# A first layer whose TensorE order is written out by hand, and W2 prepared from split parts alone

## The chip, the core and the metric

The kernel runs on one core of a Trainium2 chip. The metric is the device time of one execution in microseconds (us). Before the change it is 360.69 us, the median of 3 runs (360.64 to 360.71). Six names recur: PE is the matrix engine (TensorE), PEld its weight loads, DVE the vector engine, ACT the scalar engine, POOL GpSimd, and SP the queue that issues most DMAs.

## The reference: what is computed

Input x is 4 batches of 512 tokens of 256 float32 values. Two layers follow each other; each adds a mixer, multiplied by a gate:

```python
xn = _layernorm(x)
s = _L0_attn_ref(xn, ...)                 # xn + rmsnorm((y(xn @ W_in.T)) @ W_out.T) * norm_w
g = _silu(_L0_ffn_ref(xn, W1, W2, W3))
x = x + s * g
# the second layer: the same, with causal attention as its mixer
# _L?_ffn_ref:
hidden = jax.nn.silu(up_gate) * up_lin    # x @ W1.T, x @ W3.T, 1024 wide
hidden = fwht(hidden)                     # Walsh-Hadamard transform along the 1024
out = jnp.einsum('bsh,dh->bsd', hidden, W2)
```

The first layer's recurrence starts from zero, so its state is one product per channel, and the whole first mixer folds into one 256 x 256 matrix (`m` in the kernel).

## The kernel before, in words

**Split products.** [...] To keep precision every operand is split into a high part, the rounded value, and a low part, the rest. `split` (L59) has ACT make the high part by a cast and DVE the low part by a subtraction. A product is then three products: high x high, high x low, low x high (`mm3`, L80). Operands of 512 columns cost one instruction per 128 rows of contraction.

**Weights.** The Walsh-Hadamard transform is moved into W2 by `prep_w2` (L139): three butterfly steps on DVE over the 8 row blocks, then a product with a 128 x 128 Hadamard matrix on PE (`w2ps`), whose result is split into `w2h` and `w2l`. This is done for two halves of W2's columns in each layer. In the first layer's first half the Hadamard product takes the float32 values unsplit (`native`, with `had_f`); in the other three it takes split parts (`had`). W1 and W3 of the first layer come as four tiles `w13_0` to `w13_3`; each serves two of eight chunks of 128 hidden channels (`split_w13`, L118). `prep_m` (L187) makes `m` from `win` and `wout` (`wg`, `wi`, `mps`).

**The first layer.** `ffn` (L461) runs once for each batch. For each of 8 chunks `c` it makes two up products (`gu`, 12 instructions of 512 columns), a silu on ACT, the gating product `h` on DVE (L523), a split into `hh` and `hl`, and, later, the down product of a chunk (`down`, 12 instructions of 256 columns) into the two banks `dn`. Before, a down runs one chunk late (`defer=1`); in batch 0 all downs come at the end (`defer=NH`), since W2 isn't ready. After each chunk there are two slots, `slot(2c)` before the down and `slot(2c+1)` after it. Other work is put there by the class `Beside` (L876): one queue of generators, spread evenly over 16 slots. That work is: the gate of the batch before (`gate_all`, g0), the mixer of this batch (`mixer`, products `o`, L709), the norm and transposes of the next batch (`norm`, `xt_..tp`), in batch 1 the second layer's W2 and the products of its attention weights (`prep_second`), in batch 2 and 3 the sums for the second layer's up products, which go out to DRAM (`prep_s`), and in batch 3 the first steps of the second layer's attention. `norm` of the second layer also makes moments (L250), which POOL raises to a power and PE turns (`mrp`, L440).

**The order on each engine.** [...] The queues are filled by a scheduler that simulates the time and takes the ready instruction of the highest priority, which follows the order in the program. `after` / `issue_after` adds an order between two instructions of one engine. `line` (L66) is a switch: while `fixed` is true, every PE instruction is put behind the one before it in the program, so that PE follows the program's order. Before, it is on from the second layer on, and for the short tail of batch 3 (L548).

**PSUM.** Eight banks: three `ms` for general use, three `gu` for up products (chunk 1 of batch 0 takes the `dn` banks instead), two `dn`.

**The second layer.** `ffn_s` (L556) runs with its order written out in `places` (L1085). Each `q` has two pairs of hidden channels; L668 is the gating product of the second, L871 in `pv` adds the attention's result to xn. 

## Time and profile before

| what | value |
|---|---|
| median of 3 runs | 360.69 us |
| the profiled execution | 360.78 us |
| its span, first to last instruction | 359.0 us |
| PE busy / DVE / ACT / POOL | 352.4 / 287.5 / 197.8 / 20.8 us |
| granted TensorE clock, mean | 1.000 |
| first batch of the first layer, up products | 8.2 to 34.1 us |
| first layer, batches 1, 2, 3 start at | 51.8, 88.6, 128.6 us |
| second layer's first product of chunk work (f_0gu1z) | about 184 us |

How to read it: a group of instructions is named by line, engine, operation and tile. `f_1gu` is the up product of batch 1, `f_1dn` its down product, buffer numbers are left out. Nearly all PE instructions have the line of a helper (L70), so tiles tell them apart. "[0.33 <-ACT xt L61]" means that the engine was idle for 0.33 us, which ended when ACT's instruction of line 61 on tile xt was done. In the view of waits the columns are the total in us, how often, and the longest. The chain's rows give the start, the length and the count of a run of instructions; since matmuls overlap, the chain's lengths are from start to start, and those are the times that a product takes of PE.

### The profile page before, as it was taken

How to read it: one execution, taken by the hardware profiler on the slowest of the kernel's cores; microseconds unless marked ns; L12 is line 12 of the kernel's file. 1: busy time of each engine (PE TensorE's matmuls, PEld its weight loads, DVE VectorE, ACT ScalarE, POOL GpSimd, SP SyncE). 2: the span in 40 equal slices, each digit the busy share in tenths (PEclk: the TensorE clock that was granted, in tenths of full speed). 3: DMA queues.
4: the chain of work that ended last, by engine and by line, in shares of the span. 5: the costliest groups of instructions: out<-in, count | busy, mean ns of one | idle time of the engine just before them, and what ended most of it. 6: DMA issues, size and time to landing. Idle time of an engine off the chain costs nothing.

```text
span 359.0 us, 6278 instructions
## 1 busy us (share of the span) xinstructions
PE 352.4 (98%) x2477; PEld 328.1 (91%) x2477; DVE 287.5 (80%) x597; ACT 197.8 (55%) x373; POOL 20.8 (6%) x22
## 2 busy tenths in 40 slices
PE   8999999999999999999999999999999999999995
PEld 6878998888988898888999999999999999999995
DVE  6899648998579938998886957989669997567645
ACT  3766156266463425674467655576555676556443
POOL 2000110300020210100110001100011000000000
PEclk9999999999999999999999999999999999999999
DMA  7925000301044316656256045572554655445501
GB/s 235 341 91 206 2 1 2 99 18 60 0 157 165 150 39 233 248 180 195 105 207 263 16 190 206 203 224 103 204 179 165 207 186 204 136 151 192 197 2 58
DMA packets 16285, 52.25 MB, mean 146 GB/s; under 512 B 1633, under 2 KB 7937, under 8 KB 16257
## 3 DMA queue, kind: packets, MB, share of 16 engines
q1 hardware_dynamic: 15968, 51.60, 40.9%
q8 instruction: 19, 0.31, 0.4%
q10 hardware_dynamic: 288, 0.26, 0.2%
q14 instruction: 10, 0.07, 0.1%
HBM read 42.40 MB, written 9.45 MB: 144 GB/s over the span
## 4 chain that ended last, share of the span: by engine, by line
PE 96%; DVE 2%; ACT 1%; issue 0%; DVEq 0%
PE f_1dn L70 6%; PE f_2dn L70 6%; PE f_1gu L70 6%; PE f_0gu L70 6%; PE f_2gu L70 6%; PE f_3gu L70 6%; PE f_3dn L70 6%; PE f_0dn L70 6%; PE sc L70 4%; PE pv L70 4%; PE o L70 3%; PE v L70 3%; PE tq L70 3%; PE warm L70 2%; PE w2ps L70 1%; PE pt L70 1%
## 5 line engine op out<-in xcount | busy, mean ns | idle before, releaser
L70 PE MATMUL f_1gu<-xt,w 128*128 128x512 f32 x96 | 24.9, 397 | 0.3 <-ACT xt L61 0.3
L70 PE MATMUL f_3gu<-xt,w 128*128 128x512 f32 x96 | 25.0, 396 | 0.0
L70 PE MATMUL f_2gu<-xt,w 128*128 128x512 f32 x96 | 24.8, 395 | 0.0
L70 PE MATMUL f_0gu<-xt,w 128*128 128x512 f32 (+1 forms) x108 | 24.3, 378 | 0.0
L70 PEld LDWEIGHTS f_0gu<-xt,w 128*128 128x128 f32 x108 | 18.4, 188 | 4.4 <-issue 1.0
L70 PEld LDWEIGHTS f_1gu<-xt,w 128*128 128x128 f32 x96 | 17.0, 188 | 3.6 <-ACT xt L61 0.5
L70 PEld LDWEIGHTS f_2gu<-xt,w 128*128 128x128 f32 x96 | 17.0, 188 | 3.0
L70 PEld LDWEIGHTS f_3gu<-xt,w 128*128 128x128 f32 x96 | 17.0, 188 | 2.9
L61 ACT CAST f_2hh<-f_2h 128x512 fp32r<-128x512 f32 x16 | 9.9, 622 | 15.4 <-DVE f_2h L523 12.3
L70 PE MATMUL f_3dn<-w2l,f_3hh 128*128 128x256 f32 x64 | 17.7, 281 | 0.0
L70 PE MATMUL f_3dn<-w2h,f_3hh 128*128 128x256 f32 x64 | 17.7, 281 | 0.0
L70 PE MATMUL f_1dn<-w2l,f_1hh 128*128 128x256 f32 x64 | 17.7, 282 | 0.0
L70 PE MATMUL f_2dn<-w2h,f_2hh 128*128 128x256 f32 x64 | 17.7, 282 | 0.0
L70 PE MATMUL f_1dn<-w2h,f_1hh 128*128 128x256 f32 x64 | 17.7, 281 | 0.0
L70 PE MATMUL f_2dn<-w2l,f_2hh 128*128 128x256 f32 x64 | 17.6, 281 | 0.0
L70 PE MATMUL f_3dn<-w2h,f_3hl 128*128 128x256 f32 x64 | 17.0, 282 | 0.0
L70 PE MATMUL f_1dn<-w2h,f_1hl 128*128 128x256 f32 x64 | 17.0, 281 | 0.0
L70 PE MATMUL f_2dn<-w2h,f_2hl 128*128 128x256 f32 x64 | 16.7, 281 | 0.0
L61 ACT CAST f_3hh<-f_3h 128x512 fp32r<-128x512 f32 (+1 forms) x17 | 10.0, 594 | 10.2 <-DVE f_3h L523 6.1
L61 ACT CAST f_1hh<-f_1h 128x512 fp32r<-128x512 f32 x16 | 9.9, 622 | 9.7 <-DVE f_1h L523 6.6
L62 DVE TENSOR_TENSOR f_2hl<-f_2h,f_2hh 128x512 fp32r<-128x512 f32 x16 | 10.9, 682 | 3.9 <-ACT f_2hh L61 3.8
L70 PE MATMUL f_0dn<-w2l,f_0hh 128*128 128x256 f32 x48 | 13.7, 286 | 0.0
(487 smaller groups left out, 1147.6 us busy)
## 6 DMA issues: line engine op xcount, KB each, us to landing
sw<-s SPq DMA_DIRECT2D x32, 896.0 KB, 6.4
s<-sp SPq DMA_DIRECT2D x8, 512.0 KB, 3.8
s<-sp SPq DMA_DIRECT2D x8, 384.0 KB, 2.8
w2raw<-in_w SPq DMA_DIRECT2D x4, 512.0 KB, 5.6
sraw<-in_w SPq DMA_DIRECT2D x4, 512.0 KB, 4.3
mrb<-there SPq DMA_DIRECT2D x4, 512.0 KB, 3.7
w13raw<-in_w SPq DMA_DIRECT2D x3, 512.0 KB, 7.1
x<-in_x SPq DMA_DIRECT2D x3, 512.0 KB, 3.6
```

Of the source, the lines that this page charges most:

```text
L61: h = nc.scalar.copy(hi, src)
L62: return h, engine.tensor_tensor(lo, src, hi.bitcast(F32), ALU.subtract)
L70: ins = call(*args, **kwargs)
```

## The change

It has six parts.

1. `prep_w2`: the `native` branch goes. All four halves are split and go through `had` by two products each. `prep_w2` can be called for one half.
2. `split_by_dma` is new: ACT writes minus the rounded value into the low part, ACT writes the high part, and a DMA issued from POOL adds the source to the low part. It is used for `w13_3`, behind the silu of chunk 2, and for `win`, whose split is moved out of `prep_m` to an earlier step.
3. `mm3` orders its terms by operand: all high x high first, then all that need one side's low part, then the other's. `late` chooses the side whose low part is wanted last.
4. `Beside` takes a list of steps. In batch 0 the order is preparation (13), the next batch's norm (3), the mixer (3); before, the mixer came ahead of the norm.
5. From batch 1 on `line["fixed"]` is on, the slots follow a table (`each`), a down runs two chunks late (`defer=2`), and the last down of batches 1 and 2 is left over (`pend`) and runs behind the first up products of the next batch. The gate is two steps (silu, then the rest). `norm(1, 1)` makes its first step in batch 3.
6. In the second layer `pv`'s additions to xn are put behind the gating product last traced.

```diff
+    def split_by_dma(src, hi, lo):
+        nc.scalar.mul(lo, src, -1.0)
+        nc.scalar.copy(hi, src)
+        nc.gpsimd.dma_start(lo.bitcast(F32), src, accum_op=ALU.add)
...
-    def mm3(o, terms):
+    def mm3(o, terms, late=0):
         seq = [(l[0], r[0]) for l, r in terms]
-        for l, r in terms:
-            seq += [(l[0], r[1]), (l[1], r[0])]
+        for side in (1 - late, late):
+            seq += [(l[1 - side], r[side]) for l, r in terms]
...
-        if (layer, q) != (0, 0):
-            split(raw, hi, lo)
+        if q:
+            with after(first["silus"][2] if q == 3 else None):
+                (split_by_dma if q == 3 else split)(raw, hi, lo)
             return hi, lo
...
-            native = layer == 0 and half == 0
-            if not native:
-                bh = t4(f"w2bh_{layer}_{half}", [P, NH, P], F32R)
-                bl = t4(f"w2bl_{layer}_{half}", [P, NH, P], F32R)
-                split(cur, bh, bl)
-                yield
+            bh, bl = (t4(f"w2b{i}_{layer}_{half}", [P, NH, P], F32R) for i in "hl")
+            split(cur, bh, bl)
+            yield
...
-                if native:
-                    matmul(o, had_f, cur[:, qs, :], start=True, stop=True)
-                else:
-                    matmul(o, had, bh[:, qs, :], start=True, stop=False)
-                    matmul(o, had, bl[:, qs, :], start=False, stop=True)
+                matmul(o, had, bh[:, qs, :], start=True, stop=False)
+                matmul(o, had, bl[:, qs, :], start=False, stop=True)
...
-    def ffn(name, xT, w13, w2, slot, defer=1, spare=(), parts=1, behind=False, tail=()):
+    def ffn(name, xT, w13, w2, slot, defer=2, spare=(), parts=1, behind=False, tail=(), pend=()):
...
-                        last_up = mm3(o[:, ts_], k_pairs((wh, wl), cols, xT, ts_))
+                        last_up = mm3(o[:, ts_], k_pairs((wh, wl), cols, xT, ts_), late=int(not behind))
...
+            if c == 0:
+                for what in pend:
+                    what()
...
-        line["fixed"] = bool(tail)
-        line["last"] = last_up
+        left = [lambda q=q: down(*q) for q in queue]
+        if not behind:
+            left.pop(0)()
         for what in tail:
             what()
-        for q in queue:
-            down(*q)
-        return dn
+        if not behind and not tail:
+            return dn, left
+        for what in left:
+            what()
+        return dn, ()
...
             if i % 2:
-                for t in (i - 1, i):
-                    nc.vector.scalar_tensor_tensor(
+                with after(first["gate"]):
+                    for t in (i - 1, i):
+                        nc.vector.scalar_tensor_tensor(
...
+        win, wout = raw_m
+        wi = [t4(f"wi{i}", [P, 4, D], F32R) for i in "hl"]
+        split_by_dma(win, *wi)
+        for _ in range(4):
...
+        if b:
+            line["fixed"] = True
+            g = gated(b - 1, dn)
+        m = mixer(b)
...
+            bg = Beside([prep] * 13 + [n] * 3 + [m] * 3, 16)
...
+            steps = [
+                [g, m, w], [m, w], [m, s], [w], [w], [n], [u], [w, w],
+                [u], [n, n], [u, s], [g], [u], [s, s], [u, u], [s],
+            ]
...
+            steps = [
+                [g, m, o], [m], [m], [o], [o, p], [n], [o], [g],
+                [p], [n, n, p], [r], [p, q], [q], [r], [q], [r, q],
+            ]
...
+            tail = [run(at.tq, j) for j in range(2)]
+            steps = [
+                [g, m, p], [m], [g], [h0], [h1, x], [], [c], [t],
+                [p], [m], [p], [p], [], [], [norms[1]], [],
+            ]
+        dn, pend = ffn(f"f0_{b}", xTs[0, b], w13, w2, each(steps), tail=tail, pend=pend)
...
-            if b == 0:
-                next(norms[1])
```

In the tables g is the gate of the batch before, m the mixer, n the next batch's norm, w and u the two halves of the second layer's W2, s its attention weights (`prep_second`), o, p and q `prep_s`, r `norm(1, 0)`; h0, h1, x, c, t are steps of the attention. `o`, `p` and `q` here are names of the table, not tiles.

More of the change, by code (lines that the diff above doesn't have):

```diff
@@ L137, in load_w2, with prep_w2 @@
         return raws
-    def prep_w2(layer, raws, dst, scratch):
+    def prep_w2(layer, raws, dst, scratch, halves=range(2)):
         w2h, w2l = dst
-        for half in range(2):
+        for half in halves:
             ds_ = slice(half * P, (half + 1) * P)
@@ L185, in load_m, with prep_m @@
         return win, wout
-    def prep_m(win, wout):
+    def prep_m(wi, wout):
         cb = wp.tile([P, 4, 2, DS], F32, name="cb")
@@ L195, in prep_m @@
         wg = [t4(f"wg{i}", [P, 4, D], F32R) for i in "hl"]
-        wi = [t4(f"wi{i}", [P, 4, D], F32R) for i in "hl"]
         for c in range(4):
@@ L202, in prep_m @@
             )
-        split(win, *wi)
         yield
@@ L522, in ffn @@
             first["silu"] = nc.scalar.activation(h, gu[0], AF.Silu)
+            first.setdefault("silus", []).append(first["silu"])
             gates.append(nc.vector.tensor_tensor(h, h, gu[1], ALU.mult))
@@ L717, in mixer @@
             for j in range(2):
-                mm3(o[:, j, :], k_pairs(xT, sl(2 * i + j), m, ALLD))
+                mm3(o[:, j, :], k_pairs(xT, sl(2 * i + j), m, ALLD), late=1)
             nc.scalar.copy(osb[:, 2 * i : 2 * i + 2, :], o)
@@ L782, in tq @@
             o = psum(f"tq{b}_{j}", [P, S])
-            mm3(o, k_pairs(first["wqk"], sl(j), self.xg, ALLS))
+            mm3(o, k_pairs(first["wqk"], sl(j), self.xg, ALLS), late=1)
             split(o, self.tqs[0][:, j, :], self.tqs[1][:, j, :])
@@ L869, in pv, with __init__ @@
             if i % 2:
-                for t in (i - 1, i):
-                    nc.vector.scalar_tensor_tensor(
-                        xn[:, t, :], self.o[:, t % 2, :], self.rden[:, t : t + 1], xn[:, t, :],
-                        ALU.mult, ALU.add,
-                    )
-    class Beside:
-        def __init__(self, *tasks, slots=2 * NH):
-            self.slots = slots
-            self.gens = [g for g, _ in tasks]
-            self.total = sum(n for _, n in tasks)
-            self.done = 0
-        def step(self):
-            while self.gens:
-                try:
-                    next(self.gens[0])
-                    self.done += 1
-                    return True
-                except StopIteration:
-                    self.gens.pop(0)
-            return False
+                with after(first["gate"]):
+                    for t in (i - 1, i):
+                        nc.vector.scalar_tensor_tensor(
+                            xn[:, t, :], self.o[:, t % 2, :], self.rden[:, t : t + 1], xn[:, t, :],
+                            ALU.mult, ALU.add,
+                        )
+    class Beside:
+        def __init__(self, steps, total=0, slots=2 * NH):
+            self.steps, self.slots, self.done = steps, slots, 0
+            self.total = total or len(steps)
         def slot(self, k):
@@ L897, in slot @@
                 self.finish()
-            while self.done < self.total * (k + 1) / self.slots and self.step():
-                pass
+            while self.steps and self.done < self.total * (k + 1) / self.slots:
+                next(self.steps.pop(0))
+                self.done += 1
         def finish(self):
-            while self.step():
-                pass
+            while self.steps:
+                next(self.steps.pop(0))
     def run(f, *args):
@@ L910, in call @@
         yield
-    NORM, MIXER, W2P = 3, 3, 12
     load_x(0, 1, (nc.sync, nc.scalar))
@@ L961, in prep_first @@
         yield
-        for _ in range(4):
+        for _ in range(3):
             next(steps)
@@ L969, in prep_first @@
             yield
-        for _ in range(2):
+        win, wout = raw_m
+        wi = [t4(f"wi{i}", [P, 4, D], F32R) for i in "hl"]
+        split_by_dma(win, *wi)
+        for _ in range(4):
             next(steps)
@@ L973, in prep_first @@
         load_x(1)
-        product = prep_m(*raw_m)
+        product = prep_m(wi, wout)
         next(product)
@@ L993, in prep_second, with gated, each, slot @@
         yield
-    dn = None
-    for b in range(B):
-        tasks = []
+    def gated(b, dn):
+        add = gate(f"g0_{b}", dn, xns[0, b], xs[b])
+        yield
+        add()
+        yield
+    def each(steps):
+        def slot(k):
+            for s in steps[k]:
+                next(s)
+        return slot
+    dn, pend = None, ()
+    for b in range(B):
+        if b:
+            line["fixed"] = True
+            g = gated(b - 1, dn)
+        m = mixer(b)
+        if b + 1 < B:
+            if b:
+                load_x(b + 1)
+            n = norm(0, b + 1)
         if b == 0:
@@ L1001 @@
             next(prep)
-            tasks.append((prep, 12))
-        if b:
-            tasks.append((call(gate_all, f"g0_{b - 1}", dn, xns[0, b - 1], xs[b - 1]), 1))
-        tasks.append((mixer(b), MIXER))
-        if b + 1 < B:
-            if b:
-                load_x(b + 1)
-            if b == 2:
-                tasks.append((prep_s(0), 4))
-            tasks.append((norm(0, b + 1), NORM))
-        if b == 0:
+            bg = Beside([prep] * 13 + [n] * 3 + [m] * 3, 16)
             early = w2_tile("early0"), w2_tile("early1")
@@ L1017 @@
             ]
+            dn, pend = ffn(
+                "f0_0", xTs[0, 0], w13, w2, bg.slot, NH, spare, parts=2, behind=True
+            )
+            continue
+        tail = ()
         if b == 1:
@@ L1020 @@
             w2_1 = w2_tiles(1)
-            tasks.append((prep_w2(1, raw2_1, w2_1, t4), W2P))
-            tasks.append((prep_second(), 5))
-        if b == 2:
-            tasks += [(prep_s(1), 4), (norm(1, 0), NORM), (prep_s(2), 4)]
+            w, u = (prep_w2(1, raw2_1, w2_1, t4, (half,)) for half in range(2))
+            s = prep_second()
+            steps = [
+                [g, m, w], [m, w], [m, s], [w], [w], [n], [u], [w, w],
+                [u], [n, n], [u, s], [g], [u], [s, s], [u, u], [s],
+            ]
+        if b == 2:
+            o, p, q = (prep_s(i) for i in range(3))
+            r = norm(1, 0)
+            steps = [
+                [g, m, o], [m], [m], [o], [o, p], [n], [o], [g],
+                [p], [n, n, p], [r], [p, q], [q], [r], [q], [r, q],
+            ]
         if b == 3:
@@ L1027 @@
             at = atts[0]
-            parts = run(at.xt_half, 0), run(at.xt_half, 1), at.xt, at.scaled, at.split_sums
-            tasks += [(call(f), 1) for f in parts]
+            h0, h1, x, c, t = (
+                call(f)
+                for f in (run(at.xt_half, 0), run(at.xt_half, 1), at.xt, at.scaled, at.split_sums)
+            )
             norms = {1: norm(1, 1)}
-            tasks.append((prep_s(3), 4))
-        bg = Beside(*tasks)
-        if b == 0:
-            dn = ffn("f0_0", xTs[0, 0], w13, w2, bg.slot, NH, spare, parts=2, behind=True)
-        else:
-            tail = [run(atts[0].tq, j) for j in range(2)] if b + 1 == B else []
-            dn = ffn(f"f0_{b}", xTs[0, b], w13, w2, bg.slot, tail=tail)
-        bg.finish()
+            p = prep_s(3)
+            tail = [run(at.tq, j) for j in range(2)]
[4 more added lines that the diff above has]
+        dn, pend = ffn(f"f0_{b}", xTs[0, b], w13, w2, each(steps), tail=tail, pend=pend)
     def store(b):
@@ L1067, in pairs @@
         return one
-    line["fixed"] = True
     gate_all("g0_3", dn, xns[0, 3], xs[3])
@@ L1088 @@
         if not final:
-            if b == 0:
-                next(norms[1])
             places[0][2].append(run(next, norms[b + 1]))
```

## The prediction

> **What bounds the kernel now.** I read the page first, for the share of each engine.

> ```profile
> span 359.0 us, 6278 instructions
> ...
> PE 352.4 (98%) x2477; PEld 328.1 (91%) x2477; DVE 287.5 (80%) x597; ACT 197.8 (55%) x373; POOL 20.8 (6%) x22
> ```

> PE is busy 98% of the span, and the page's clock row is 9 throughout, so the clock is not in question. A busy PE can still hide waits. So I took the view of waits next, for PE alone. It is complete:

> ```profile
> PE warm L70 <- DVE zr L924: 1.4, 1, 1.4
> PE f_0gu2z L70 <- DVE f_0h L668: 0.6, 1, 0.6
> PE f_1gu L70 <- ACT xt L61: 0.3, 1, 0.3
> ```

> Beyond the start there are two waits, 0.9 us together. PE sets the end (96% of the chain), so only two things can shorten the kernel: fewer PE microseconds, or those two waits. Anything that makes PE wait once more lengthens it by the same amount. In the first layer from its second batch on, which the change reorders by hand, PE has no wait inside the batches at all (51.8 to 170 us: busy throughout). That part of the change can gain next to nothing there.

> The chain of waits gives prices on PE. The first fence is of the first batch, the second of the second.

> ```profile
> 18.22 0.86 PE w2ps L70 x2
> 19.07 1.40 PE f_0gu L70 x6
> 20.48 0.86 PE w2ps L70 x2
> ```
> ```profile
> 73.34 0.47 PE w2ps L70 x2
> ```

> Two records of w2ps on the unsplit `had_f` are one product of 512 columns in full float32: 0.86 us. Six products of split parts take 1.40, so 0.233 each; two from splits are 0.47. A product of 256 columns is 0.95/8 = 0.118 (f_1dn).

> **The change, part by part.**

> *W2 from splits.* Half 0 loses two native products (2 x 0.86 = 1.72) and gets four from splits (4 x 0.233 = 0.93): -0.78 us of PE. As PE has no idle time there, it comes off the end if the other engines keep up. The new split of `cur` costs ACT 1.05 and DVE 1.21 (the rows of the other half: w2bh at 24.79, w2bl at 26.67).

> *Two lower parts by DMA.* w13_3 and win lose a DVE subtraction each (1.22 and 1.21) and gain an ACT pass each (1.05). Net in the first batch: DVE +1.21 - 2.43 = -1.2, ACT +1.05 + 2.10 = +3.2. Here are the windows of that batch (columns: PE, weight loads, DVE, ACT, POOL):

> ```profile
> 18.00:27.00 9.00, 9.00 (x36) 6.59 (x36) 9.00 (x17) 5.77 (x11) 0.00 (x0) 1.00 0.31 93
> 27.00:34.00 7.00, 7.00 (x35) 5.81 (x34) 7.00 (x12) 5.05 (x10) 0.00 (x0) 1.00 0.74 258
> ```

> DVE is full for 16 us and ACT has 5.2 free, so 3.2 more fits by sum. By order it is less comfortable. The extra split falls at about 19, while the subtractions that go were at 25.41 and 30.59. So DVE is up to 1.21 late in between. Who waits: three gu banks rotate (chunk 1 uses dn), so chunk 5's first product needs chunk 3's gating, done 22.75 for a start at 23.97: 1.2 to spare. Chunks 6 and 7 have 1.3 and 1.0. PE is also up to 0.78 earlier. Bounds 0 to 1.2 (1.21 + 0.78 less the spare 1.2 would be 0.8; 1.2 if ACT's gating functions slip too); I take +0.3, because the scheduler may still put the gatings first.

> *When the DMA must land.* Chunk 6 starts at 26.77 and its lower-weight products come last of each sum, 4 x 0.233 later; less 0.78 this is 26.9. Before, DVE delivered the part with nothing to spare:

> ```profile
> 25.41 1.22 DVE L62 TENSOR_TENSOR w<-w13raw,w 128x1024 fp32r<-128x1024 f32 x1
> ```

> After, ACT negates behind chunk 2's gating function (ends 18.05). ACT's first gap of 1.05 is before the row at 21.37 (idle 1.15), so the negation ends between 19.1 (at once) and 23.0 (behind that row), say 21.4. No row shows an accumulating DMA or one issued from POOL. The nearest rows are SP's 512 KB loads: x 3.6, sraw 4.3, win 8.7 under the opening load. The DMA engines are 0.31 busy here, so I take 4.3: it lands at 25.7, 1.2 in time. [...] This trace has POOL rows beside DVE: a 128x4 power takes 1.01 at 40.73 with DVE idle and 1.51 and 1.91 at 64.13 and 65.66 with DVE busy. [...] I take the row, 0, with ends 0 and 4.8 (8.7 us from 23.0). win's DMA lands in the same way, for mps products that before started at 31.4.

> POOL's queue: ln_1r at 40.73 and ssr at 48.59 stand behind these two issues, 10 us later. 0. The raw tiles are held until the DMAs end; w2bh, wi and wg take the next of ten buffers. 0, inside the ends above. SP issues `load_x(1)` a slot or two later: x1 landed well before bn_stats at 34.73, which waited for no DMA. 0.

> *End of the first batch.* The norm's transposes are moved ahead of the mixer. Before, they were spread among the last downs, and the next batch waited for their copy:

> ```profile
> 50.98 0.36 PE L70 MATMUL f_0dn<-w2l,f_0hh 128*128 128x256 f32 x1
> 51.18 0.28 PE L70 MATMUL f_0dn<-w2h,f_0hl 128*128 128x256 f32 x1
> 51.79 0.73 PE L70 MATMUL f_1gu<-xt,w 128*128 128x512 f32 x2 [0.33 <-ACT xt L61]
> ```

> From 51.18 to 51.79 is 0.61 where 0.12 is normal (0.49), and the next product, started at once, lost 0.10. xn was ready at 43.2, so transposes can stand 7 us earlier, under the 96 downs (11.3 us). Then `late=1` asks for the lower x last. Gain 0 to 0.59, I take -0.45. What is late next is the mixer's row (L729 ended 52.6), which nobody needs before the gating.

> *The fixed order of batches 1 to 3.* Its PE sum is unchanged. `defer=2` gives each down one chunk more; the first down of a batch comes 7 us or more after the gating that frees dn. In batch 1, up to the transposes of slot 9, PE has five chunks (14.0), three downs (4.2), the mixer (2.8) and four w2ps (0.9): 22.0 us. DVE has five gatings and four lower parts (9 x 0.67), five butterfly steps (5 x 1.28), the mixer (3.1), one W2 split (1.2), the norm (3.4) and two w2l (1.3): 21.4. So DVE has no reserve, but a bank that PE needs is freed 2.8 us (one chunk) before its turn. Tightest is batch 2: slot 13 starts the moments (DVE 1.39 + 0.5 + 0.2, POOL 1.0 to 1.9), slot 15 transposes them on PE one chunk (2.8) and one down (1.42) later: 4.2 of room for 3.1 to 4.5 and whatever DVE is behind. Before, mrp stood at 130.43, 2.6 after its power ended, and moved freely. Behind mrp are queued the last downs and all of batch 3, so its wait counts whole. Bounds: 0 to 1.5 over all three batches; below nothing is excluded, as PE never waited. I take +0.4.

> *pv's addition behind the gating.* In the second layer PE waited 0.6 for L668 (195.22). The DVE timeline shows what stood before it:

> ```profile
> 193.00 0.69 DVE L62 TENSOR_TENSOR f_0hl<-f_0h,f_0hh 128x512 fp32r<-128x512 f32 x1 [0.69 <-ACT f_0hh L61]
> 193.61 0.87 DVE L871 SCALAR_TENSOR_TENSOR xn<-pv,rden,xn 128x256 f32<-128x256 f32 x2
> 194.40 0.68 DVE L668 TENSOR_TENSOR f_0h<-f_0h,f_0gu1l 128x512 f32<-128x512 f32 x1
> ```

> Its silu had ended at 193.47, so L668 can start 0.79 earlier. The start-to-start excess of the PE there is 0.76. Next late would be the bank of pv, wanted by the second transposes at about 195.3; the additions end at 195.2. Gain 0 to 0.76; I take -0.65.

> The reordered sums, norm(1,1) one step earlier and the other moves leave PE's count alone: 0.

> **Sum.** The profiled execution took 360.78 (span 359.0 and 1.8 around it), 0.09 above the median 360.69. 360.78 - 0.78 - 0.45 - 0.65 + 0.3 + 0.4 = 359.6; less 0.09, 359.5.

> **Rivals.** What the measurement can tell from no change is about 0.2%, 0.72 us.
> - A, forecast (0.55): the gains arrive, new waits stay under 1.2. With all gains whole and no new wait it is 360.69 - 2.13 = 358.5; so 358.5 to 359.9, likeliest 359.5.
> - B, waits trade places (0.21): PE saves 0.78, but the copy of xt_1 or the fixed order (mrp, slots of batch 1 where DVE has no reserve) takes 1.2 to 2.6: 360.0 to 361.4, typically 360.5. For it: DVE full in those stretches. Against: no PE wait there before and more room for the downs. To it belongs that reordering does nothing, 360.69 - 0.78 = 359.9, plus one small wait.
> - C, slower (0.24): the lower part of w13_3 lands late for chunk 6. It costs from a landing at 26.9 on, and outweighs the forecast's net gain of 1.2 by more than 0.72 once the stall passes 1.9: a landing after 28.8, 5.8 us from 23.0. Full price 4.8: 359.5 + 4.8 = 364.3; half way 361.9. For it: DVE is full, and nothing can fill PE before W2 is ready. Against: 4.3 us is the likelier transfer.

> The range leaves out C's far half (0.12) and 0.05 around A's lower end: 358.4 to 361.9. Faster 0.55, within 0.21, slower 0.24.

> **What would show it.** Right: four w2ps of 0.233 per half; no PE wait at the first product of batch 1 nor at gu2z; the two POOL transfers landing before chunk 6. Wrong: a PE wait for w or w13 by a DMA at about 26 to 29 us, a PE wait at mrp or at any first-layer gu product, or an f_0gu group that starts later than before.

## The result, and the profile after

The changed kernel takes 375.31 us, the median of 6 runs (373.88 to 375.95), against 360.61 for the kernel before. The ratio is 1.0401, 95% interval 1.0378 to 1.0425. That is far outside the predicted range, and on the other side. The top of the page, in which PE's count of instructions is the same as before:

```profile
span 373.1 us, 6284 instructions
...
PE 358.6 (96%) x2477; PEld 331.9 (89%) x2477; DVE 287.1 (77%) x596; ACT 201.9 (54%) x376; POOL 21.0 (6%) x24
...
PEclk9999999889999789999999999999999999999999
```

PE is "busy" 6.2 us longer for the same count of instructions, and the clock row has dents in two places. Before, it was

```profile
PEclk9999999999999999999999999999999999999999
```

The view of waits for PE (who waited for whom: total, times, longest) gives the rest. It replaces the three lines shown of before:

```profile
PE xt_2tp L76 <- DVE xn L277: 3.5, 1, 3.5
PE xt_3tp L76 <- DVE xn L277: 2.6, 1, 2.6
PE w2ps L76 <- DVE w2bl L62: 1.8, 1, 1.8
PE warm L76 <- DVE zr L918: 1.5, 1, 1.5
PE f_2dn L76 <- DVE f_2hl L62: 0.6, 1, 0.6
PE w2ps L76 <- ACT w2bh L61: 0.2, 1, 0.2
```

The two waits of before are gone (gu2z for L668, f_1gu for xt). Four new ones, 8.5 us, stand in batches 1 and 2, all for DVE; a fifth, of 0.2 us, is in batch 0. The windows view of those stretches (PE, PEld, DVE, ACT, POOL busy; then the granted clock) shows what follows a wait:

```profile
68.24:71.65 3.41, 1.65 (x7) 1.24 (x7) 3.41 (x7) 1.52 (x4) 0.00 (x0) 1.00 0.00 0
71.65:75.06 3.41, 3.41 (x9) 2.64 (x8) 3.41 (x10) 1.24 (x4) 0.00 (x0) 0.50 0.00 0
78.47:81.89 3.42, 1.50 (x9) 1.04 (x10) 3.42 (x8) 2.25 (x3) 0.00 (x0) 1.00 0.22 74
81.89:85.30 3.41, 3.41 (x11) 2.64 (x10) 3.39 (x4) 1.42 (x3) 0.00 (x0) 0.50 0.20 79
122.85:126.26 3.41, 1.45 (x10) 1.25 (x10) 3.04 (x13) 2.13 (x3) 1.43 (x1) 1.00 0.00 0
126.26:133.09 6.83, 5.66 (x17) 4.46 (x18) 6.83 (x18) 3.05 (x6) 1.81 (x2) 0.50 0.77 262
```

Behind the three stretches in which PE was busy for 1.65, 1.50 and 1.45 us of 3.41, the granted clock is 0.50 for 3.41, 3.41 and 6.83 us. In the slow stretches PE was busy 12.5 us, so some 6.2 us are lost there (an estimate: half of it).

The excess of PE makes an account. It is the time from each product's start to the next one's start, less the product's own price (0.233 for 512 columns, 0.118 for 256, 0.108 for a transpose record). The four records of before's unsplit w2ps are priced at 0.233 as well, so 0.8 us of their own higher price stand in its 3.75. Kernels e1 to e12 are told below.

| stretch (us) | before | after | e1 | e2 | e5 | e7 | e9 | e12 | e11 |
|---|---|---|---|---|---|---|---|---|---|
| to the last up of batch 0 | 3.75 | 3.51 | 3.46 | 3.67 | 3.73 | 3.30 | 3.44 | 3.50 | 3.55 |
| to the last up of batch 1 | 0.79 | 9.71 | 1.93 | 6.21 | 2.10 | 1.33 | 1.33 | 0.17 | 14.91 |
| to the last up of batch 2 | 0.08 | 6.59 | 1.92 | 6.03 | 0.23 | 0.23 | 0.23 | 1.93 | 9.38 |
| to the last up of batch 3 | 0.01 | 0.10 | 0.06 | 0.13 | 8.40 | 8.78 | 3.85 | 0.06 | 0.94 |
| second layer, from f_0gu1z | 1.92 | 0.65 | 0.62 | 0.62 | 0.60 | 0.58 | 0.61 | 0.60 | 1.28 |

After less before: +8.9 in batch 1, +6.5 in batch 2, -0.2 in batch 0, -1.3 in the second layer, 14.0 in all. The spans differ by 14.1.

Where was DVE when PE waited for xn? Its timeline in the changed kernel, and POOL's row in the same stretch:

```profile
76.21 0.18 DVE L274 TENSOR_SCALAR ln_2r<-ln_2mv 128x4 f32<-128x4 f32 x1
...
77.48 0.70 DVE L159 TENSOR_TENSOR w2b<-w2b 128x512 f32<-128x512 f32 x1
78.08 0.70 DVE L160 TENSOR_TENSOR w2b<-w2b 128x512 f32<-128x512 f32 x1
78.68 1.24 DVE L62 TENSOR_TENSOR qkl<-qkraw,qkh 128x1024 fp32r<-128x1024 f32 x1
79.82 1.40 DVE L277 TENSOR_SCALAR xn<-x,ln_2mv,ln_2r 128x256 f32<-128x256 f32 x4
```
```profile
76.47 1.38 POOL L275 TENSOR_TENSOR ln_2r<-ln_2r,mhalf 128x4 f32<-128x4 f32 x1 [14.71 <-DVE ln_2r L274]
```

PE has stood since 76.9, at the transpose that is next in its order: it was busy for 0.01 us of the 3.50 up to 80.4. Until 77.85 xn has to wait for POOL's power. But then DVE goes on with a butterfly and the split of qk, which the table places in slot 10, ahead of the norm that the transposes of slot 9 need: 2.0 us. The rest of the delay is older, since the norm's first row (ln_2st) stands at 67.57, and at 61.38 before. In the kernel before, xn came 9.8 us earlier:

```profile
70.02 1.37 DVE L278 TENSOR_SCALAR xn<-x,ln_2mv,ln_2r 128x256 f32<-128x256 f32 x4
```

### The profile page after: what moved, and what is told of

It reads as the page before. It is cut to its first block, busy times and chain, and to the rows that moved or that the text cites. A ratio compares the mean times of both kernels' runs of the same rounds, so it can differ in the third digit from the quotient of the medians.

```text
span 373.1 us, 6284 instructions
## 1 busy us (share of the span) xinstructions
PE 358.6 (96%) x2477; PEld 331.9 (89%) x2477; DVE 287.1 (77%) x596; ACT 201.9 (54%) x376; POOL 21.0 (6%) x24
## 3 DMA queue, kind: packets, MB, share of 16 engines
q0 software_dynamic: 288, 1.05, 1.7%
## 4 chain that ended last, share of the span: by engine, by line
PE 85%; DVE 11%; ACT 2%; issue 1%; DVEq 0%
PE f_0dn L76 6%; PE f_3gu L76 6%; PE f_3dn L76 6%; PE f_0gu L76 5%; PE f_1dn L76 5%; PE f_2dn L76 5%; PE sc L76 4%; PE pv L76 4%; PE f_2gu L76 3%; PE f_1gu L76 3%; PE v L76 3%; PE tq L76 3%; PE o L76 2%; PE warm L76 1%; DVE osb L733 1%
## 5 line engine op out<-in xcount | busy, mean ns | idle before, releaser
L76 PE MATMUL f_1gu<-xt,w 128*128 128x512 f32 x96 | 26.7, 434 | 0.0
L76 PEld LDWEIGHTS f_1gu<-xt,w 128*128 128x128 f32 x96 | 19.9, 212 | 4.6
L76 PE MATMUL f_3gu<-xt,w 128*128 128x512 f32 x96 | 23.7, 396 | 0.0
L76 PEld LDWEIGHTS f_2gu<-xt,w 128*128 128x128 f32 x96 | 18.8, 202 | 4.1
L61 ACT CAST f_1hh<-f_1h 128x512 fp32r<-128x512 f32 x16 | 9.9, 621 | 16.9 <-DVE f_1h L527 13.8
L61 ACT CAST f_2hh<-f_2h 128x512 fp32r<-128x512 f32 x16 | 9.9, 621 | 16.2 <-DVE f_2h L527 13.0
L76 PE MATMUL f_2dn<-w2h,f_2hl 128*128 128x256 f32 x64 | 18.0, 281 | 0.6 <-DVE f_2hl L62 0.6
L76 PE MATMUL f_3dn<-w2h,f_3hl 128*128 128x256 f32 x64 | 18.0, 281 | 0.0
L76 PE MATMUL f_1dn<-w2h,f_1hl 128*128 128x256 f32 x64 | 17.9, 280 | 0.0
L61 ACT CAST f_3hh<-f_3h 128x512 fp32r<-128x512 f32 (+1 forms) x17 | 10.0, 596 | 12.3 <-DVE f_3h L527 8.1
L62 DVE TENSOR_TENSOR f_2hl<-f_2h,f_2hh 128x512 fp32r<-128x512 f32 x16 | 11.0, 688 | 4.2 <-ACT f_2hh L61 4.1
L62 DVE TENSOR_TENSOR f_3hl<-f_3h,f_3hh 128x512 fp32r<-128x512 f32 (+1 forms) x17 | 11.1, 655 | 3.9 <-ACT f_3hh L61 3.8
```

The lines of the kernel that those rows point to most:

```text
L61: h = nc.scalar.copy(hi, src)
L62: return h, engine.tensor_tensor(lo, src, hi.bitcast(F32), ALU.subtract)
L76: ins = call(*args, **kwargs)
```

## The experiments

**Theories.** 1: PE's order is fixed, but DVE's is still picked by the scheduler, which takes any ready work (1a: of later slots) ahead of what the fixed PE waits for. 2: the first batch's edits, or the DMA from POOL, put DVE behind. 3: the mixer of batch 0, moved behind the norm, slides its DVE tail into batch 1. 4: the table itself asks for W2 before the norm.

**e1, PE's order free again.** `line["fixed"] = True` is moved from the loop over batches to the second layer.

> The changed kernel with the fixed PE order taken away in batches 1 to 3 of the first layer; table, defer=2, W2 from splits and DMAs stay. Theory 1 (PE's order is fixed while DVE's is still chosen by the scheduler, so PE stands before transposes whose input DVE makes late): PE waits in the first layer under 1 us in all, no row of the clock under 9, 359 to 361 us. Theory 2 (the edits of the first batch, or the DMA from POOL, put DVE behind): waits of 3 us or more stay, over 367. Theory 3 (only the mixer's move in batch 0 puts DVE behind): about the same as without the edit in DVE's backlog, 362 to 370.

362.34 us, ratio 1.0049 (1.0034 to 1.0064); the clock is whole. 13.0 of the 14.7 us go with this one line: theory 1, and theory 2 (over 367) falls. But the time is above theory 1's 359 to 361, at the low end of theory 3's range, and the waits left are 2.4 us, more than the 1 that was expected:

```profile
PE f_2gu L76 <- DVE f_2h L527: 0.9, 1, 0.9
PE f_1dn L76 <- DVE f_1hl L62: 0.9, 1, 0.9
PE f_2dn L76 <- DVE f_2hl L62: 0.4, 1, 0.4
```

**e2, the mixer ahead of the norm.** `[prep] * 13 + [m] * 3 + [n] * 3`.

> The changed kernel with batch 0's mixer ahead of the next batch's norm again, as before the change. Theory 3 (the mixer's DVE tail, 2.9 us, slid into batch 1 and is what makes it late): batch 1's waits fall from 5.6 to under 2.7 us and its lost clock (3.7) to under 2, so 368 to 371 us; batch 2's waits of 3.5 stay. Theory 1 (the order of DVE's queue, with any work as filler): the waits of batch 1 fall by at most 1, over 373 us.

371.62 us, 1.0306 (1.0286 to 1.0325). The wait before w2ps and the clock lost behind it are gone, 3.5 us in batch 1. The wait before xt_2tp has grown from 3.5 to 4.1, where theory 3 had expected under 2.7 for the whole batch, and batch 2 keeps its own. The time lies between the two expectations. So theory 3 is a quarter of it.

**e3, PE kept busy.** Unused products ahead of the waiting steps:

```diff
+    def filler(xT, n):
+        o = psum("fill", [P, S])
+        for i in range(n):
+            matmul(o, had, xT[0][:, i % 2, :], start=True, stop=True)
```

> The changed kernel with 8, 16 and 14 products (233 ns each, results unused) ahead of the waiting w2ps and transposes of batches 1 and 2, so that PE is busy while DVE catches up; nothing it waits for comes earlier. If the lost clock (about 7 us in the records after the waits) comes from PE's idle time, it goes and the kernel takes 367 to 370 us although PE does 8.8 us more. If the clock falls for another reason, or the fill only adds, 375 to 384 us.

372.97 us, 1.0333 (1.0305 to 1.036). That is 2.3 us less than the changed kernel takes, though PE has 8.8 us more to do, but above the 367 to 370 that were expected. In batch 2 the clock stays whole and 2.1 us are won. In batch 1 xt_2tp starts at 80.4 as in the changed kernel, since DVE sets it, and the clock still falls:

```profile
78.79:82.20 3.41, 2.18 (x12) 1.22 (x11) 3.41 (x8) 2.47 (x3) 0.00 (x0) 1.00 0.35 94
82.20:85.61 3.41, 3.41 (x10) 2.65 (x9) 3.17 (x4) 1.19 (x3) 0.00 (x0) 0.50 0.15 60
```

In batch 2, then, it was PE's idle time that had cost the clock. In batch 1 a wait of 1.2 us and eight transpose records in one window, with PE busy for 2.18 us of 3.41, were enough.

**e4, W2 from splits and pv's order, on the kernel before.**

> The kernel before with two parts alone: W2's first half from splits as well, and pv's additions behind the gating product. By the prediction's steps -0.78 and -0.65 (up to -1.3 by the second layer's rows after): 358.5 to 359.6 us. Rival: DVE, full in the first batch, gives the 0.78 back (359.6 to 360.3).

360.11 us, 0.9989 (0.9982 to 0.9996), in the rival's range. In batch 0 PE now waits for DVE's gating and ACT's cast of win, 0.5 us and more, and its excess is 0.7 above before.

**e5, later work behind the norm.**

```diff
         def slot(k):
-            for s in steps[k]:
-                next(s)
+            with after(first["scaled"] if k > 5 and len(steps[5]) else None):
+                for s in steps[k]:
+                    next(s)
```

> The changed kernel; in batches 1 and 2 all DVE work of the table's slots 6 and later is put behind the next batch's norm (its last row, xn), and nothing else is changed. Theory 1a (work of later slots, which depends on nothing on PE, is taken ahead of the norm that PE's fixed order waits for): xn comes some 6 us earlier in batch 1, the waits before xt_2tp and xt_3tp fall under 1.2 us, that before w2ps to about 0.8 (it has the mixer's slid tail ahead of it), lost clock under 2: 362 to 366 us. Theory 3 (the slid mixer tail alone) or 2 (the first batch): waits before xt_2tp of over 2.5 and before xt_3tp as they were, over 370.

369.71 us, 1.0253 (1.0236 to 1.027), outside what was expected, yet the two batches do what theory 1a says: xn starts at 71.8 (79.8 in the changed kernel), and PE's waits for DVE before w2ps and xt_3tp are gone. What was won came back as one new wait:

```profile
PE mrp L76 <- POOL mr L259: 6.8, 1, 6.8
PE warm L76 <- DVE zr L918: 1.5, 1, 1.5
PE xt_2tp L76 <- DVE w2l L62: 1.1, 1, 1.1
```

It is in the main the edit's own. The second layer's norm and its moments (slots 10 and 13 of batch 2) are put behind xn as well, and PE has mrp fixed in slot 15. The norm's statistics begin 24.8 us after the batch's first product (17.6 in the changed kernel), and the power on the moments ends 43.0 us after it (36.4), when PE has stood ready since 36.2. In e6, which has no such pin and a wait of only 0.2 us in batch 2, it ends after 35.1, and mrp waits for nothing.

**e6, another table.** The norm's first step in slot 2, W2's first half behind it:

```diff
-                [g, m, w], [m, w], [m, s], [w], [w], [n], [u], [w, w],
-                [u], [n, n], [u, s], [g], [u], [s, s], [u, u], [s],
+                [g, m], [m], [m, n, s], [w], [w], [w], [w], [],
+                [u], [n, n], [w, w, s], [g, u], [u], [s, s, u], [], [s, u, u],
...
-                [g, m, o], [m], [m], [o], [o, p], [n], [o], [g],
-                [p], [n, n, p], [r], [p, q], [q], [r], [q], [r, q],
+                [g, m, o], [m], [m, n], [o], [o], [p], [o], [g],
+                [p], [n, n], [r, p], [p, q], [q], [r], [q], [r, q],
```

> The changed kernel with another table for batches 1 and 2: the next batch's norm three slots earlier, at slot 2, W2's first half behind it with its w2ps at slot 10, all PE steps of the norm where they were. Theory 4 (the table asks for W2 before the norm; order in the table is what counts): no PE wait over 1 us, 360 to 364 us. Theory 1a (the scheduler still takes butterflies of later slots while the norm waits for POOL's power): w2ps's wait of 1.8 goes, xt_2tp's stays over 1.5 and xt_3tp's over 1, 366 to 372 us.

366.95 us, 1.0176 (1.0153 to 1.02). More than half of the loss goes. The wait for xn shrinks to 0.8, but PE waits 3.1 for `f_1hl` instead, and the clock falls for 6.8 us. The time lies in the range of theory 1a, but not for the reason given: the waits of over 1.5 and over 1 before the transposes did not come. The table's order matters, but it does not by itself decide DVE's.

**e7, e5 and e2 together.**

> The changed kernel with later slots' DVE work behind the norm, as in e5, and batch 0's mixer ahead of the norm, as in e2. If these two are the whole of DVE's lateness: PE waits in the first layer under 1 us in all, the clock whole, 359 to 361 us. If something else stays (the first batch's edits, the two-chunk delay): waits of 2 us or more, over 363.

368.9 us, 1.0228 (1.0213 to 1.0243). Batch 1 is down to 1.33 of excess and batch 2 to 0.23. What keeps it from the expected 359 to 361 is mrp's wait of 6.7, which stays with the pin.

**e8, W2 from splits, the two DMAs and pv's order, on the kernel before.** The mixer stays ahead of the norm, and `mm3` keeps its order.

> The kernel before with W2's first half from splits, the two lower parts by DMA and pv's additions behind the gating product; order, table and mixer as before the change. With the DMAs DVE has 2.4 us less in the first batch than in e4, so the 0.7 us that e4 lost there come back: 358.7 to 359.6 us. Rival (ACT's added passes take it back): 359.7 to 360.5.

360.5 us, 0.9997 (0.9989 to 1.0006). The expectation missed. The time is at the upper end of the rival's range, but not for the rival's reason: batch 0 has no wait beyond the start. PE waits 1.0 us in three places of the later batches, all for DVE, the longest:

```profile
PE f_3dn L76 <- DVE f_3hl L62: 0.5, 1, 0.5
```

**e9, e7 with mrp in batch 3.** `[r, q]` becomes `[q]` in batch 2's last slot and batch 3's second slot is `[m, r]`.

> e7 with the one wait that was left moved: the turn of the moments (mrp) from batch 2's last slot to slot 1 of batch 3. Theory 1 (PE's fixed order waits for what DVE delivers late, and nothing else is wrong): the wait of 6.7 and the lost clock behind it go, PE waits under 1.5 us in the first layer, 359 to 361 us. Rival (DVE is behind in batch 2 whatever stands there, and the wait moves on to batch 3's transposes or gu products): over 363.

363.21 us, 1.0071 (1.0055 to 1.0088). 5.7 us of e7's go, but the rival is partly right: two waits of 0.8 and 0.9 before f_2dn come up in mrp's place, with one slow stretch of 3.41.

**e10, pv's order alone, on the kernel before.**

> The kernel before with one part alone, pv's additions behind the gating product. The second layer is laid down by hand and does not move with the first: -1.2 us as its rows lost in the changed kernel (excess of PE over its products 1.92 before, 0.65 after), 359.2 to 359.7 us. Rival (only the 0.65 of the prediction): 359.8 to 360.1; (the scheduler reorders the first layer for it): over 360.3.

359.3 us, 0.9964 (0.9951 to 0.9976). It is faster than both kernels. The excess of the second layer is 0.69 (1.92 before), 0.8 of the gain in its first batch and the rest in the three others.

**e11, a fixed PE order alone, on the kernel before.** `line["fixed"] = b > 0` at the head of the loop; the line that turned it off is gone.

> The kernel before with one part alone: PE in program order from batch 1 on, with the old queue of side work and one chunk of delay. Theory 1 (a fixed PE order beside a DVE order that the scheduler picks is enough): PE waits of 3 us or more in the first layer and lost clock, over 365 us. Rival (it is the table, the two-chunk delay or the slid mixer that makes PE wait): under 362.

383.64 us, 1.0635 (1.0617 to 1.0653).

```profile
PE xt_2tp L70 <- DVE xn L278: 9.8, 1, 9.8
PE xt_3tp L70 <- DVE xn L278: 5.5, 1, 5.5
```

The fixed order is enough without table, delay, W2 or DMA. It waits in the same two places, and the changed kernel, with its table, is 8.3 us below it.

**e12, e1 and e2 together.**

> e1 (PE's order free in batches 1 to 3) with batch 0's mixer ahead of the norm. If e1's remaining waits (2.4 us before f_1dn, f_1gu, f_2dn, f_2gu) come from the mixer's tail, they halve and it is under 361.3; otherwise 362 to 362.6.

360.73 us, 1.0004 (0.9995 to 1.0013), as expected from the mixer's tail. Batch 1's waits are gone, batch 2's 1.3 us stay.

**What follows.** Theory 1 is shown from both sides: e1 takes the fixed order away and 13.0 us go, e11 adds it alone and 23.1 come. 1a is shown for the two waits it names by e5. Theory 3 is worth 3.7 us by e2 with the order fixed and 1.6 by e12 with it free. Theory 4 is a part (e6). What stays open is whether any table with a fixed PE order can be faster here: e9, the nearest, still waits for ACT and DVE, and a fixed DVE order beside it was not tried.

## Why the prediction was wrong, step by step

- **"The fixed order of batches 1 to 3 ... Bounds: 0 to 1.5 ... I take +0.4"** is the step that failed. The sum of DVE's work up to slot 9 (21.4 us for PE's 22.0) was made as if DVE followed the table. It doesn't: from the first gating of batch 1 at 54.18 DVE is full until xn starts at 79.82, 25.6 us. In them stand 2.9 us of batch 0's mixer (L733, L736) and some 4.7 us of slots that lie behind the transposes in the table: the third butterfly step (1.2), the split of qk (1.1) and the gate's two products and two additions (2.4), which ran at 61.17 and 65.77 though the table has them in slot 11. The other 18 us are work that the sum had listed. What spoke against a larger loss was that PE had never waited there before. But then its order came out of the same simulation as DVE's, and that reason is void once one of the two is fixed.
- **"The mixer's row ... which nobody needs before the gating"**: priced at 0, cost 3.7 us (e2). The row itself is not waited for; the work is, since DVE had room at the end of batch 0 (in the kernel before, busy for 2.46 us of the 8.80 from 43.0 on) and is full in batch 1 of the changed one (25.64 of 25.64 us from 54.18 on). Moved work has to be priced where it lands.
- **"Anything that makes PE wait once more lengthens it by the same amount"**: no. 8.5 us of waits brought another 7 with them, an estimated 6.2 of it from the clock (0.50 in the slow stretches). I set the clock aside since its row was 9 throughout; that row only says that PE had never stood long (0.6 us at most, behind the start).
- **Tightest is mrp**: in the changed kernel it was not. mrp ran at 143.79, 6.1 us after its power had ended. The tight places were w2ps and the transposes. The 6.8 us of e5 don't settle it, since that edit itself held the moments back; e6 has 2.7 us to spare there.
- **The first batch, -0.78, -0.45, +0.3**: batch 1 started at 51.11 instead of 51.79, -0.68 for -0.93. Of this, 0.29 stood already at the first up product (7.87 instead of 8.16), of which none of the three terms speaks. The w2ps cost 0.233 each and the wait for xt is gone. A wait of 0.24 for the new w2bh took part back, 0.51 with the late starts around it (two w2ps began 0.64 and 0.34 behind the record before them, for 0.233 each). On the kernel before, the W2 edit loses its gain altogether (e4 is 0.8 above e10).
- **The DMA for chunk 6**: right, with 0 cost, in part by luck: it was issued at 18.97, well before the 21.4 of the forecast, and took 5.3 us for 4.3. So it landed at 24.3, for a forecast of 25.7 and a need at about 27; win's took 5.7. No wait for w shows. So rival C had its price on a resource that was fine. That the two took 5.3 and 5.7 for the 4.3 of the row for sraw is not explained: DVE was full beside both (busy for 5.27 of 5.30 us and 5.67 of 5.70), and no run has such a transfer beside an idle DVE. The powers on POOL that the prediction lists (1.01 beside an idle DVE, 1.51 and 1.91 beside a busy one) are no transfers, and what they mean for one was not shown.
- **pv behind the gating, -0.65**: right in kind, half in size; it gives 1.25 (e10). By the excess, 0.80 of it is in the second layer's first batch and 0.43 in the three others, which the term had left out.

The rivals held no case of this size: B allowed 2.6 us for the fixed order, C took its loss from the DMA.

## What to carry to other kernels

If one engine's queue is fixed by hand and the others' are picked by a scheduler, the fixed engine waits for whatever the others put first; fix or pin the producers of what it waits for, or leave both free. Before work is moved, ask whether the engine that does it has room where it lands, not whether someone waits for its result. On a kernel bound by PE a wait can cost more than its length: in the changed kernel a slow stretch at a granted clock of 0.50 came behind each of the waits of 1.8, 3.5 and 2.6 us, while one of 1.1 in e5 had none. Until the clock row after it is known, count half of such a stretch on top (an estimate from that clock: 1.7 us for one of 3.41).

## What the runs showed of the hardware

```profile
75.06:78.47 3.41, 1.82 (x14) 1.56 (x12) 3.41 (x8) 1.55 (x2) 1.38 (x1) 1.00 0.00 0
```
```profile
128.62:132.04 3.42, 1.73 (x13) 1.32 (x12) 3.42 (x14) 1.83 (x3) 0.00 (x0) 1.00 0.62 241
132.04:135.45 3.41, 3.41 (x13) 2.93 (x12) 2.92 (x9) 0.62 (x1) 1.34 (x1) 0.50 0.56 220
```

Up to the end of the products there are 12 drops from full clock. Ahead of 11 of them PE was busy for 1.73 us or less of the window. In all windows at full clock without a drop behind them it was busy for 1.82 us or more. The twelfth drop is e3's, behind 2.18 us, of which 1.49 were transposes. So in these traces a drop goes with PE's share of a window (1.73 of 3.41 is 0.51, 1.82 is 0.53), and not with the length of one wait: two waits of 0.8 and 0.9 us in one window cost clock in e9, while 0.9 us in e1 and 1.1 us in e5 left PE 2.53 and 2.34 us of work in theirs and cost none. In the changed kernel 1.76 us without PE work in one window (3.41 less 1.65) was enough. No run varied this share by itself, nor the part that transposes have in it, so why e3's window lost the clock is not shown.
